# The sums of a graph layer's edge rows on TensorE: two places moved within a stage

## The chip, the cores and the metric

The kernel runs on one core of one Trainium2 chip. The metric is the time of one execution in device microseconds; the figure for the kernel before is the median of three runs. A core has five engines with a list of instructions each: PE (TensorE, matrix products, written to PSUM), DVE (VectorE), ACT (ScalarE), POOL (GpSimd) and SP (SyncE). SP issues most of the loads, POOL issues the indirect writes. The engines wait for each other through semaphores; each goes through its own list in order.

## The reference

A graph layer with 6250 nodes of 64 features and 206250 edges (100000 random ones in both directions, and a loop at each node), sorted by their target. Each edge has 64 features of its own. For each edge a two-layer network is applied to the features of one end and of the edge, the results are averaged over the edges of each source node (`row`), and a second network with a residual and a layer norm follows:

```python
msg = jnp.concatenate([src_node_features[col], edge_attr], axis=1)
h = jax.nn.relu(msg @ W1a.T + b1a)
h = h @ W1b.T + b1b
sums = jax.ops.segment_sum(h, row, num_segments=n_nodes)
...
agg = sums / jnp.maximum(counts, 1.0)[:, None]
z = jnp.concatenate([src_node_features, agg], axis=1)
z = jax.nn.relu(z @ W2a.T + b2a)
z = z @ W2b.T + b2b
out = jnp.concatenate([z, src_node_features], axis=1) @ Wr.T + br
...
x = _layernorm(x + out, axis=-1)
```

## The kernel before

The edges are padded to 1612 tiles of 128 and cut into 124 groups of 13 tiles. The source nodes fall into 49 bins of 128. The kernel sorts the hidden rows of the edges (128 values, a one for the count, and the node's place in its bin) by bin into a table in HBM, reads the table back bin by bin, and sums the rows of a bin with a one-hot matrix of the node numbers on PE. The second layer of the edge network is applied after the sum, since it is linear.

The main loop (`for k, ep_ in enumerate(epoch_of)`) has one **stage** for each group k. Several groups are in the making at once: in stage k the hidden rows of group k are computed, the places of group k+1 in the table are found, the one-hots of group k+2 are made, the inputs of group k+3 are loaded, and the rows of group k-2 are written.

In stages 8 to 103 a part of the group's tiles (6 of 13, or 9 in every other stage from 9 to 25) goes another way, the **joins**: three tiles at a time are first sorted within SBUF by a matmul with marks (one-hots of places), so that four rows of one bin lie side by side and can be written with one descriptor. Such a stage has two joins (or three). The names, with the lines of the profile:

- `counts_of(k+1)` on PE (L1092, L1093, L1096): how many edges of each bin stand ahead. It writes the PSUM tile `cnt_ps`.
- `hidden(k, ...)` on PE (L1353): first-layer rows of the tiles outside the joins, in two parts, `parts` and `last_part`. ACT takes them from PSUM (L1356) into `orow`.
- `join_bases(k+1)` on DVE (L1106 `of_quads`, L1110 `bases`): from the counts, the first place of each bin in the joins.
- `join_ranks(k+1)` on PE (L1119, L1121, L1122, L1127, L1131): the ranks of the next joins' edges. It needs `of_quads` and `bases`. The instructions `slots` (L1195, L1202), `join_at_slots` (L1143 `z_act`, L1144) and `join_places` (L1153, L1161, L1165) on DVE read what it left; in DVE's list they stand behind `marks`, `bins_of` and `side`, and L1195 is the first that waits for L1131.
- `marks(k, i)` on DVE (L1233) and ACT (L1238, L1239): the one-hots of join i. `side(k+1, ...)` on ACT (L1247) and DVE (L1250, L1254): the operands to be sorted.
- `join(k, i)` on PE (L1265), 6 matmuls of 512 columns: the sorting. ACT copies the result to SBUF (L1270 `rj`).
- `join_rows(k, i)` on PE (L1278): first-layer rows of the sorted edges; ACT takes them from PSUM (L1281). It needs `rj`. Between the copies and these evictions ACT's list has `columns(k+2, 1)` (L1318).
- `scatter(k-2)` on POOL (L1393 single rows, L1364 four rows at a time): the indirect writes. Some of them are made to wait for a matmul of the running stage (`pace`).
- `nodes_ahead`, `nodes_residual`, `nodes_load`, `nodes_store`: 17 small pieces of the node network, in stages 9 to 59, every third stage.

The **sums** of the table run while it is still being filled, on the part of each bin that is complete. Their work is cut into sum groups of up to three bins and twelve tiles, and `groups_at[k]` holds those of stage k: one, sometimes two, in a stage with joins. None is due before stage 29. A sum group goes through `issue` (the reads of the table, L1455 on SP, up to nine buffers ahead), `mark` (the one-hots, L1484 on DVE), and the matmuls of `summed` (L1503), into one PSUM tile (`h_ps`). `collect` adds the PSUM tile to `part` (L1563 on DVE, or for a bin's first sum a copy, L1561 on ACT), one sum group later. The first sum group of a stage is done in two pieces: `sum_first(k)` sums the first two of three bins, `sum_rest(k, g)` the other one, and then marks the next sum group and collects the last one. Further sum groups of the stage follow at its end with `sum_next(k)`. In the profile one f32 tile shows as two matmul records.

All tiles named `h_ps` share five PSUM buffers. The lists of PE, ACT, DVE and SP have the order in which the loop issues the instructions (`manual_schedule`); POOL's list is made by the compiler's scheduler. So on PE a stage with joins has the order: counts of k+1, first hidden rows of k, ranks of k+1, small node pieces, `sum_first`, last hidden rows, two joins, rows of the joins (with a third join between them where there is one), `sum_rest`, further sum groups.

Of the kernel before, what the change touches and what calls it, by code (L numbers as in the profile page):

```python
# [487 lines left out]
def fast_path(  # L488
# [64 lines left out]
    def joined(k):  # L553
        if not JOIN_FROM <= k < JOIN_TO:
            return 0
        return 3 if k in THRICE else 2
# [194 lines left out]
    with (  # L751
# [741 lines left out]
        def summed(st, reads, oh, of_bin, bins=None):  # L1493

            at_tile = 0
            for b0, nb, t0, n, rt in reads:
                for j in range(nb):
                    b = b0 + j
                    if bins and b not in bins:
                        at_tile += n  # L1500
                        continue
                    for t in range(n):
                        m = nc.tensor.matmul(  # L1503
                            of_bin(b), oh[:, at_tile, :], rt[:, j * n + t, : H + 1],
                            start=t0 + t == st.lo[b], stop=t0 + t == st.hi[b] - 1,
                        )
                        at_tile += 1
            return m.ins.name
# [36 lines left out]
        def mark():  # L1545

            if issued:
                g = issued.pop(0)
                g.oh = nodes_of(g.st, g.reads)
                marked.append(g)  # L1550
# [14 lines left out]
        def sum_first(k):  # L1565

            if not marked:
                mark()
            g = marked.pop(0)
            g.ps = hp.tile([P, SUMS, H + 1], F32, name="h_ps")  # L1570
            g.half = range(g.b0, g.b0 + -(-g.nb // 2))
            done[k, "first"] = summed(g.st, g.reads, g.oh, lambda b: g.ps[:, b - g.b0, :], g.half)
            return g

        def sum_rest(k, g):
            if g.nb > len(g.half):
                done[k, "rest"] = summed(
                    g.st, g.reads, g.oh, lambda b: g.ps[:, b - g.b0, :], range(g.half.stop, g.b0 + g.nb)
                )
            totals.append(g)  # L1580
            mark()
            collect(1)
            return g
# [27 lines left out]
        def issue(k):  # L1611

            while to_issue and sum(len(g.reads) for g in issued + marked) + len(to_issue[0][1]) <= READS:
                issued.append(Sums(k, *to_issue.pop(0)))
# [70 lines left out]
        for k, ep_ in enumerate(epoch_of):  # L1685
# [7 lines left out]
            due = len(issued) + len(marked) + len(to_issue)  # L1693
# [40 lines left out]
            if k + 2 < NGR:  # L1734
                columns(k + 2)
                ahead = bins_of(k + 2)
            if after:
                join_ranks(k + 1)
                side(k + 1, 1)
# [45 lines left out]
                nodes_load(nodes_at[k + 1])  # L1785
            if k in clears:
                clear(*clears[k])
            issue(k)

            g = sum_first(k) if due > 0 else None  # L1790
            if k + 1 < NGR:
                slots(k + 1, counts)
            if after:
# [6 lines left out]
                columns(k + 2, 1)  # L1800
            if after:
                join_places(k + 1)
            for i in range(joined(k)):
                join_rows(k, i)
                if i + 2 < joined(k):
                    join(k, i + 2)
            made.pop(k)
            if g:
                sum_rest(k, g)
                issue(k)  # L1810
            if k >= LEAD:
                scatter(k - LEAD)
            for i in range(1, due):
# [199 lines left out]
```

## Time and profile before

| | |
|---|---|
| median of 3 runs | 2145.13 us (2137.46 to 2148.65) |
| the profiled execution | 2149.18 us, of which the span of its instructions is 2147.2 us |
| mean granted clock of PE | 0.867 |
| PE, DVE, POOL, ACT busy | 76%, 63%, 54%, 51% of the span |
| stages 29 to 103 (joins and sums) | 448.2 to 1556.8 us of the span |

The page lists busy shares, the span in slices, the DMA queues, the chain of waits that ended last, and the groups of instructions of one line and shape. A group's row has the line and engine, the operation, the tile written and those read, the shape, the count, then busy time, the mean length in ns, and the idle time of that engine just before these instructions with what ended it. The timeline gives start, length, engine, line and, in brackets, the idle time before. The view of waits gives, for an engine and line, the instruction it waited for, the sum in us, how often and the longest. The windows give the same counts for a stretch of the span. "issue" and "remote" stand for waits whose end the profile does not show. Ends of matmuls are modelled, and a few records of matmuls are missing.

### The profile page before, as it was taken

What the parts mean: (1) busy time and instruction counts of PE and PEld (TensorE: products, weight loads), DVE (VectorE), ACT (ScalarE), POOL (GpSimd) and SP (SyncE); (2) the same over time, 40 slices, a digit from 0 to 9 for tenths busy, and PEclk for the clock granted to TensorE, in tenths of its full rate; (3) what the DMA queues carried; (4) which work ended last, traced back from release to release, by engine and by line L of the source; (5) the groups of instructions that cost most, each with busy time, mean ns of one, the idle gap of its engine ahead of it and who ended that gap; (6) DMA issues with size and microseconds to landing.
All of it is one profiled execution on the core that took longest, in us unless ns stands there. A gap on an engine that the chain in (4) does not pass through costs nothing.

```text
span 2147.2 us, 32795 instructions
## 1 busy us (share of the span) xinstructions
PE 1636.0 (76%) x10759; PEld 1443.4 (67%) x10759; DVE 1352.7 (63%) x3111; ACT 1087.4 (51%) x2203; POOL 1168.9 (54%) x1238
## 2 busy tenths in 40 slices
PE   4648776778888788888878878887767777777777
PEld 4536665667777677777767767776656666666666
DVE  7256666667766677767767767777645344454367
ACT  1237776766676566666666666666622222222015
POOL 5565565656665555556555565665654544545420
PEclk8568898999999999989998999999978777888889
DMA  7566666666765656555555555555677555565563
GB/s 183 151 204 201 214 226 209 232 210 208 226 206 182 199 174 199 171 150 183 176 157 157 170 159 175 180 172 162 196 224 219 165 173 165 171 187 162 159 180 104
DMA packets 227514, 394.09 MB, mean 184 GB/s; under 512 B 43228, under 2 KB 162527, under 8 KB 226951
## 3 DMA queue, kind: packets, MB, share of 16 engines
q1 hardware_dynamic: 152837, 224.58, 37.4%
q0 software_dynamic: 48368, 120.75, 16.2%
q10 hardware_dynamic: 26130, 46.58, 6.3%
q8 instruction: 88, 1.44, 0.3%
q14 instruction: 91, 0.75, 0.1%
HBM read 217.82 MB, written 173.91 MB: 182 GB/s over the span
## 4 chain that ended last, share of the span: by engine, by line
PE 59%; ACT 12%; issue 11%; another core or an unknown queue 9%; DVE 7%; DMA 2%; DVEq 0%; ACTq 0%; POOL 0%; SPq 0%; POOLq 0%
PE h_ps L1503 23%; PE h_ps L1353 10%; PE h_ps L1265 9%; PE h_ps L1278 8%; ACT orow L1356 2%; ACT rj L1270 2%; ACT rhs L1318 2%; ACT marks L1238 1%; ACT rhs L1316 1%; DVE marks L1233 1%; DMA rt<-rows 1%; PE cnt_ps L1092 1%; PE cnt_ps L1093 1%; ACT marks L1239 1%
## 5 line engine op out<-in xcount | busy, mean ns | idle before, releaser
L1393 POOL DMA_INDIRECT rows<-orow,rowidx x1009 | 973.1, 964 | 811.9 <-issue 211.3
L1503 PE MATMUL h_ps<-rt,oh 128*128 128x129 f32 x4014 | 601.9, 301 | 141.6 <-issue 135.7
L1503 PEld LDWEIGHTS h_ps<-rt,oh 128*128 128x128 f32 x4014 | 549.7, 214 | 170.9 <-issue 168.6
L1356 ACT ACTIVATE orow<-h_ps 128x384 f32<-128x384 f32 (+1 forms) x295 | 157.1, 536 | 727.1 <-PE h_ps L1353 501.1
L1278 PE MATMUL h_ps<-mv,rj 128*128 128x130 f32 x1608 | 260.9, 317 | 152.7 <-ACT rj L1270 98.3
L1278 PEld LDWEIGHTS h_ps<-mv,rj 128*128 128x128 f32 x1608 | 235.3, 220 | 191.8 <-ACT rj L1270 115.6
L1265 PE MATMUL h_ps<-marks,side 128*128 128x512 f32 x1206 | 322.5, 414 | 31.2 <-ACT orow L1356 10.3
L1353 PE MATMUL h_ps<-mv,rhs 124*128 124x128 f32 x2018 | 309.2, 301 | 33.5 <-issue 17.7
L1563 DVE TENSOR_TENSOR part<-part,h_ps 128x387 f32<-128x387 f32 (+2 forms) x219 | 111.6, 510 | 352.1 <-remote 172.4
L1484 DVE TENSOR_TENSOR oh<-ramp,rt 128x768 f32<-128x768 bf16 (+3 forms) x428 | 315.0, 775 | 4.6 <-DMA rt<-rows 4.6
L1353 PEld LDWEIGHTS h_ps<-mv,rhs 124*128 124x128 f32 x2018 | 280.0, 213 | 41.0 <-issue 21.6
L1265 PEld LDWEIGHTS h_ps<-marks,side 128*128 128x128 f32 x1206 | 227.8, 197 | 84.9 <-ACT orow L1356 12.3
L1233 DVE TENSOR_TENSOR marks<-quad_ramp,ramp 128x1024 fp32r<-128x1024 f32 x201 | 241.2, 1204 | 0.0
L1364 POOL DMA_INDIRECT quads<-orow,qidx x201 | 192.8, 959 | 78.5 <-issue 36.9
L1281 ACT ACTIVATE orow<-h_ps 128x260 f32<-128x260 f32 x402 | 138.5, 388 | 69.5 <-PE h_ps L1278 32.6
L1270 ACT COPY rj<-h_ps 128x512 f32<-128x512 f32 x201 | 113.8, 588 | 111.1 <-PE h_ps L1265 67.9
L1106 DVE TENSOR_SCALAR of_quads<-cnt_ps 128x98 bf16<-128x98 f32 x96 | 25.5, 266 | 229.1 <-PE cnt_ps L1096 84.5
L1239 ACT ACTIVATE marks<-marks,ones 128x512 fp32r<-128x512 f32 x201 | 145.2, 722 | 6.6
L1050 DVE TENSOR_TENSOR_SCAN had<-ramp,bins 128x400 bf16<-128x400 bf16 (+1 forms) x124 | 137.5, 1109 | 12.4 <-issue 0.3
L1238 ACT ACTIVATE marks<-quad_ramp,z_act 128x512 fp32r<-128x512 f32 x201 | 143.7, 715 | 0.0
L1316 ACT ACTIVATE rhs<-rhs,from_win 60x896 f32<-60x896 bf16 (+1 forms) x116 | 130.4, 1124 | 2.9
L1318 ACT ACTIVATE rhs<-rhs,ones 60x896 f32<-60x896 f32 (+1 forms) x116 | 130.2, 1123 | 2.9
(188 smaller groups left out, 1505.0 us busy)
## 6 DMA issues: line engine op xcount, KB each, us to landing
rt<-quads SPq DMA_DIRECT2D x113, 390.0 KB
rt<-rows SPq DMA_DIRECT2D x100, 390.0 KB
rt<-rows SPq DMA_DIRECT2D x115, 195.0 KB
rhs<-in_edgeT SPq DMA_DIRECT2D x87, 224.0 KB
enat<-in_edgeJ SPq DMA_DIRECT2D x87, 192.0 KB
rows<-orow,rowidx POOLq DMA_INDIRECT x1009
quads<-padrow ACTq DMA_DIRECT2D x12, 1300.0 KB
rt<-rows SPq DMA_DIRECT2D x45, 325.0 KB
```

Of the source, the lines that this page charges most:

```text
L1233: nc.vector.tensor_tensor(m[:, :n, :], all_q[:, None, :].to_broadcast([P, n, QUAD * P]), z[:, :n, None].to_broadcast([P, n, QUAD * P]), op ...
L1238: nc.scalar.activation(m[:, t, :], all_q, AF.Square, bias=z_acts[k][:, i * JOIN + t : i * JOIN + t + 1], scale=-1.0)
L1239: nc.scalar.activation(m[:, t, :], m[:, t, :], AF.Relu, bias=ones[:, :1], scale=-1.0)
L1265: nc.tensor.matmul(ps, s[:, p, i * JOIN + t, :], m[:, t, :], start=t + p == 0, stop=t == JOIN - 1 and p == 1,)
L1278: done[k, f"join{i}"] = nc.tensor.matmul(ps[:, j, :], rj[:, (g0 + j) * P : (g0 + j + 1) * P], m, start=True, stop=True).ins.name
L1318: nc.scalar.activation(rhs[D:WIDE, :], rhs[D:WIDE, :], AF.Relu, bias=ones[D:WIDE, :1], scale=-1.0)
L1353: done[k, c] = nc.tensor.matmul(ps[:, j, :], rhs[:WIDE, of * P : (of + 1) * P], m[:WIDE, :H], start=True, stop=True).ins.name
L1356: nc.scalar.activation(orow_of(k, k0, n)[:, :, :H], ps[:, :n, :], AF.Relu)
L1364: s = nc.gpsimd.indirect_dma_start(out=qep.rows.rearrange("(q r) f -> q (r f)", r=QUAD), out_offset=bass.IndirectOffsetOnAxis(ap=qidx[:, q ...
L1393: s = nc.gpsimd.indirect_dma_start(out=ep_.rows, out_offset=bass.IndirectOffsetOnAxis(ap=rowidx[:, k % RING * BLK + j : k % RING * BLK + j ...
L1484: nc.vector.tensor_tensor(res[:, at_tile : at_tile + nb * n, :], ramp[:, None, :].to_broadcast([P, nb * n, P]), node[:, :, None].to_broadc ...
L1503: m = nc.tensor.matmul(of_bin(b), oh[:, at_tile, :], rt[:, j * n + t, : H + 1], start=t0 + t == st.lo[b], stop=t0 + t == st.hi[b] - 1,)
```

## The change

Three calls move within a stage; no other line changes. The first reads of the sums (`issue(k)`) and `sum_first(k)` go from behind the node pieces to ahead of the next joins' ranks. `sum_rest(k, g)`, with the marking and collecting in it, and the second `issue(k)` go from behind the joins' rows to between the first two joins and their rows.

```diff
                 columns(k + 2)
                 ahead = bins_of(k + 2)
+            issue(k)
+            g = sum_first(k) if due > 0 else None
             if after:
                 join_ranks(k + 1)
                 side(k + 1, 1)
...
             if k in clears:
                 clear(*clears[k])
-            issue(k)
-
-            g = sum_first(k) if due > 0 else None
             if k + 1 < NGR:
                 slots(k + 1, counts)
...
             if after:
                 join_places(k + 1)
+            if g:
+                sum_rest(k, g)
+                issue(k)
             for i in range(joined(k)):
                 join_rows(k, i)
                 if i + 2 < joined(k):
                     join(k, i + 2)
             made.pop(k)
-            if g:
-                sum_rest(k, g)
-                issue(k)
             if k >= LEAD:
                 scatter(k - LEAD)
```

On PE the order of a stage with joins becomes: counts of k+1, first hidden rows of k, `sum_first`, ranks of k+1, node pieces, last hidden rows, two joins, `sum_rest`, rows of the joins, further sum groups. In stages without joins PE's order is the same as before. On DVE the order stays but for the first stage with a sum, where the one-hots come ahead of L1250 and L1254. On ACT the copies L1561 come ahead of that stage's evictions L1281. On SP the reads L1455 come ahead of the node pieces' loads and stores. On POOL four pairs of neighbouring writes change places.

## The prediction

> **What bounds the kernel now.** I read the page first: busy shares, then the chain of waits.
>
> ```profile
> span 2147.2 us, 32795 instructions
> ...
> PE 1636.0 (76%) x10759; PEld 1443.4 (67%) x10759; DVE 1352.7 (63%) x3111; ACT 1087.4 (51%) x2203; POOL 1168.9 (54%) x1238
> ...
> PE 59%; ACT 12%; issue 11%; another core or an unknown queue 9%; DVE 7%; DMA 2%; DVEq 0%; ACTq 0%; POOL 0%; SPq 0%; POOLq 0%
> ```
>
> PE carries 59% of the chain and is busy 76% of the span. An average says nothing about where a moved matmul matters, so next I asked in which stretch the moved instructions (L1503) and the joins' ranks (L1119) run together. Columns: window, length, PE busy (count), PEld busy, granted clock, DMA share, GB/s. The first three rows hold L1503 alone, the fourth all engines.
>
> ```profile
> 0.00:448.20 448.20, 0.00 (x0) 0.00 (x0) 0.81 0.66 206
> 448.20:1556.80 1108.60, 272.78 (x1924) 255.14 (x1924) 0.93 0.59 180
> 1556.80:2147.20 590.40, 329.15 (x2092) 294.54 (x2091) 0.80 0.59 173
> ```
>
> ```profile
> 448.20:1556.80 1108.60, 904.95 (x6204) 800.55 (x6202) 790.17 (x1882) 702.28 (x1384) 659.09 (x686) 0.93 0.59 180
> ```
>
> No sums run before 448.2 (stage 29), and after 1556.8 (stage 104 on) there are no joins, so nothing stands between the two new places and the old ones: hidden rows follow the first bins and other bins follow the hidden rows in both orders. Only 1108.6 us, 75 stages of 14.8 us, can change. PE is idle there for 1108.6 - 904.95 = 203.7 us. The groups of instructions name what it waited in front of (last part of a row: idle time before it, and its causes):
>
> ```profile
> L1278 PE MATMUL h_ps<-mv,rj 128*128 128x130 f32 x1202 | 195.4, 314 | 111.7 <-ACT rj L1270 58.4 <-issue 24.1 <-ACT orow L1281 20.2
> L1119 PE MATMUL cnt_ps<-joh,before_w 128*128 128x300 bf16 x74 | 22.6, 305 | 48.0 <-DVE of_quads L1106 45.0 <-issue 2.6
> L1503 PE MATMUL h_ps<-rt,oh 128*128 128x129 f32 x1924 | 273.0, 297 | 6.9 <-issue 6.6 <-ACT orow L1281 0.3
> ```
>
> So 111.7 + 48.0 = 159.7 of the 203.7 us stand exactly at the two places to which sums are moved, and the sums themselves almost never wait for their data (6.9 us). One stage on PE's timeline (start, length, then the idle time before):
>
> ```profile
> 1022.71 1.12 PE L1353 MATMUL h_ps<-mv,rhs 124*128 124x128 f32 x8
> 1025.37 0.29 PE L1119 MATMUL cnt_ps<-joh,before_w 128*128 128x300 bf16 x1 [1.53 <-DVE of_quads L1106]
> ...
> 1026.19 1.59 PE L1503 MATMUL h_ps<-rt,oh 128*128 128x129 f32 x12
> 1027.61 0.83 PE L1353 MATMUL h_ps<-mv,rhs 124*128 124x128 f32 x6
> 1028.20 2.99 PE L1265 MATMUL h_ps<-marks,side 128*128 128x512 f32 x12
> 1031.03 1.55 PE L1278 MATMUL h_ps<-mv,rj 128*128 128x130 f32 x12
> 1033.34 0.71 PE L1278 MATMUL h_ps<-mv,rj 128*128 128x130 f32 x4 [0.76 <-ACT rhs L1318]
> 1033.89 0.83 PE L1503 MATMUL h_ps<-rt,oh 128*128 128x129 f32 x6
> 1034.56 0.33 PE L1092 MATMUL cnt_ps<-had,one_w 128*128 128x400 bf16 x1
> ```
>
> PE goes through its list in order: it stands for DVE's `of_quads` with 12 sum matmuls ready behind the ranks, and for ACT with 6 ready behind the rows.
>
> **The change part by part.** No instruction is added or removed.
>
> *First bins in front of the ranks.* They occupy PE from 1026.19 to the next start, 1027.61: 1.42 us. In front of L1119 that covers each wait up to 1.42 us. The waits, by releaser (sum, times, longest):
>
> ```profile
> PE cnt_ps L1119 <- DVE of_quads L1106: 45.0, 31, 3.9
> PE h_ps L1278 <- ACT rj L1270: 58.4, 29, 3.9
> PE h_ps L1278 <- ACT orow L1281: 20.2, 29, 0.8
> ```
>
> With the 2.6 us put to "issue" there are 48.0 us in some 33 waits. Upper bound: 33 x 1.42 = 47. Lower bound, if all were 3.9 or nothing: 48.0 / 3.9 = 12 waits x 1.42 = 17. The mean wait (1.45) is about the cover; I take 34.
>
> *Other bins between joins and rows.* From 1033.89 to 1034.56: 0.67 us. The rows' end is set by ACT (the copy L1270, then L1318, then the evictions L1281), counted from the joins' end, so it stays where it is and the next stage starts 0.67 us sooner wherever ACT makes PE wait at least that long. The 29 waits for L1270 (mean 2.0) and the 29 for L1281 (mean 0.70) give 58 x 0.67 = 39; every one of 75 stages would give 50. I take 45.
>
> *Sum and what is left of it.* 34 + 45 = 79 us (56 to 97 by the bounds). Not all of it arrives, for a stage cannot get shorter than what the other engines need. In the window DVE has 790.17 / 75 = 10.5 us a stage, ACT 9.4, and POOL:
>
> ```profile
> 1031.28 0.96 POOL L1393 DMA_INDIRECT rows<-orow,rowidx  x1 [0.31 <-issue]
> ```
>
> 0.96 + 0.31 = 1.27 us an instruction, 686 of them: 871 us, 11.6 a stage. The mean stage (14.8) has room for 1.05 us; the short one above (12.3) has not, and where a late `rj` also holds back the evictions the next wait grows. I take 0.6 of 79: 47 us; the ends for the range are 0 and 1.
>
> *Clock.* PE's rows show a second price of standing still:
>
> ```profile
> 1098.20 0.41 PE L1119 MATMUL cnt_ps<-joh,before_w 128*128 128x300 bf16 x1 [2.36 <-DVE of_quads L1106]
> ...
> 1099.27 2.93 PE L1503 MATMUL h_ps<-rt,oh 128*128 128x129 f32 x12
> 1101.99 1.49 PE L1353 MATMUL h_ps<-mv,rhs 124*128 124x128 f32 x6
> ```
>
> Behind that stop the same 12 matmuls take 2.72 us, not 1.42. Over the window the grant is 0.93, so (1 - 0.93) x 1108.6 = 78 us are lost. The stops become shorter, but a stop of 3.9 us only by 1.42 or 0.67; I take 10 of the 78 (0 to 60). The Trainium skill ("TensorE: Matmul & The Clock Gate", "What's actually happening") gives the rule: one idle window of about 3.4 us halves the clock, and it is binary. The factor of 1.9 in these rows agrees; that a shorter stop of 2.36 us was enough differs from a plain threshold, since the window may lie anywhere.
>
> *What is pushed back.* (a) In the 74 - 33 = 41 stages without a wait at L1119 the ranks now start 1.42 us later. DVE's L1195 waits for the last rank matmul (L1131), and behind it in DVE's list stand `z_act`, `join_places`, the one-hots and the next marks.
>
> ```profile
> 1009.53 0.18 PE L1131 MATMUL cnt_ps<-of_quads,more_w 128*128 128x50 bf16 x1
> 1013.30 0.52 DVE L1195 TENSOR_REDUCE row<-cnt_ps 128x7 f32<-128x350 f32 x1
> L1195 DVE TENSOR_REDUCE row<-cnt_ps 128x7 f32<-128x350 f32 (+1 forms) x76 | 39.8, 524 | 16.2 <-PE h_ps L1265 9.1 <-remote 4.7 <-issue 2.4
> ```
>
> DVE comes 3.6 us after the ranks; 2.2 would remain: nothing lost, though if that cover were gone it would cost 41 x 1.42 = 58 us. (b) The first ACT copies of 17 sum groups (L1561) come in front of the row evictions:
>
> ```profile
> L1561 ACT COPY part<-h_ps 128x387 f32<-128x387 f32 (+1 forms) x17 | 7.7, 469 | 4.9 <-PE h_ps L1353 3.5 <-PE h_ps L1503 1.4
> ```
>
> at most 7.7 us; the 0.67 us of sums cover most, I take 2. (c) On SP the reads for the sums come in front of the node groups' loads and stores (17 each); nobody waits for the stores, the reads come sooner: 0, within 3 us either way. (d) POOL's list keeps its order but for four neighbouring pairs: 0. (e) In stages with two sum groups DVE's addition L1563 waits for the other bins, which now end before the rows:
>
> ```profile
> 1023.45 0.56 DVE L1563 TENSOR_TENSOR part<-part,h_ps 128x387 f32<-128x387 f32 x1 [4.62 <-PE cnt_ps L1096]
> ```
>
> That wait was what made the marks and `of_quads` late for 1025.37. It helps where the cover is too short, at most the 48 - 34 = 14 us left there; I take 0.
>
> Total 47 + 10 - 2 = 55. The profiled execution took 2149.18 us (span 2147.2 and 2.0 around it): 2094. The median of the runs is 4 us lower than it, 2145.13, so I forecast **2090 us**.
>
> **The rivals.** *Nothing arrives:* the waits turn up again further on (at L1353 for PSUM, at L1265 for marks), because ACT and POOL, not PE, pace the stages. For it: POOL's 11.6 us, the chain's 12% ACT and 9% unknown. Against: those engines are idle for a fifth or more of each stage. With a tenth of the 55 us left: 2140. Chance 0.13.
>
> *The clock stays up:* with the stops cut, most of the 78 us come back: 60 in place of 10, 2040. For it: the two rows of L1503, a factor of 1.9. Against: the stops of 2 to 4 us lose only 0.67 or 1.42. By the rule of the Trainium skill just named a longest stop of 3.9 - 0.67 = 3.2 us falls short of a window. Chance 0.12.
>
> *Slower:* the ranks in the 41 stages come too late for DVE. PE's signals sometimes arrive long after the matmul: L1356 wants the hidden rows of 1010.98 and starts at 1016.02.
>
> ```profile
> 1010.98 0.83 PE L1353 MATMUL h_ps<-mv,rhs 124*128 124x128 f32 x6
> 1016.02 0.49 ACT L1356 ACTIVATE orow<-h_ps 128x384 f32<-128x384 f32 x1 [2.06 <-PE h_ps L1265]
> ```
>
> From the point where the ranks' signal is over 2.2 us late the delay goes through DVE's list into the next joins. Price up to 58, less 0.6 x 45 = 27 still gained at the rows: 2145 + 31 = 2176. Against: only 16.2 us of waiting at L1195 today. Chance 0.18.
>
> That the change does not do what it says is excluded: the changed program has the moved matmuls in the new places in all 75 stages.
>
> **How the numbers follow.** Forecast 0.57 (its own range 2065 to 2120), nothing 0.13, clock 0.12, slower 0.18. Range 2038 to 2160: it holds the forecast, the second case and parts of the two outer ones, with under 0.2 outside. About 0.5%, 11 us, is what this kernel's runs can tell from no change: below 2134 lie the forecast and the clock, less a tail, 0.68; 2134 to 2156 holds "nothing" and a little of its neighbours, 0.14; above, 0.18.
>
> **What would show it.** Right: idle before L1119 falls from 48.0 to under 20, before L1278 from 111.7 to about 70, the window to stage 104 is some 55 us shorter and the time after it is still 590 us. Clock: a grant over 0.93 in the window. Wrong: idle before L1195 well over 16.2 us (the slower rival), or new idle time before L1353, L1265 or L1503 that adds up to what L1119 and L1278 lost.

## The result and the profile after

The changed kernel is slower by 1%: its median is 2162.27 us against 2141.3 us for the kernel before, run beside it, ratio 1.0104 with a 95% interval of 1.0067 to 1.0140. One of its six runs, at 2867.64 us, lies far above the others and is left out of the ratio. The profiled execution of the changed kernel (2154.23 us) is its fastest run, while that of the kernel before (2149.18 us) is above all its timed runs, so the two traces differ by 5 us only, and their parts say more than their sums.

The windows of the changed kernel, cut where the sums begin and at the same place behind stage 104 as before (window, length, busy time of PE, PEld, DVE, ACT, POOL with counts, granted clock, DMA share, GB/s):

```profile
0.00:449.00 449.00, 302.30 (x1718) 254.86 (x1719) 268.76 (x679) 242.57 (x492) 260.49 (x292) 0.79 0.65 205
449.00:1565.70 1116.70, 917.36 (x6214) 809.38 (x6212) 790.90 (x1882) 697.38 (x1383) 659.89 (x686) 0.91 0.58 178
1565.70:2152.40 586.70, 435.05 (x2832) 393.24 (x2830) 293.21 (x552) 145.31 (x330) 249.94 (x261) 0.79 0.59 175
...
449.00:1554.30 1105.30, 908.69 (x6150) 802.08 (x6148) 784.78 (x1872) 693.25 (x1374) 653.19 (x679) 0.91 0.58 178
```

The middle window was to get 55 us shorter and got 8 us longer (1108.6 before). It holds stage 104 too; from here on "the stages" are exactly 29 to 103 (fourth row), which took 1097.2 us before and 1105.3 us after. The outer windows moved by less than 4 us. The groups of these stages in the changed kernel (busy, mean ns, then idle time before them and its causes):

```profile
L1278 PE MATMUL h_ps<-mv,rj 128*128 128x130 f32 x1202 | 196.3, 313 | 125.7 <-ACT rj L1270 80.4 <-issue 25.9 <-ACT orow L1281 15.2
L1265 PE MATMUL h_ps<-marks,side 128*128 128x512 f32 x900 | 247.2, 424 | 45.0 <-DVE xr_now L1660 14.6 <-DVE nz L1652 9.1 <-ACT xr_now L1653 7.9
L1119 PE MATMUL cnt_ps<-joh,before_w 128*128 128x300 bf16 x74 | 22.1, 299 | 11.1 <-DVE of_quads L1106 8.2 <-issue 2.8
L1270 ACT COPY rj<-h_ps 128x512 f32<-128x512 f32 x150 | 83.9, 588 | 129.5 <-PE h_ps L1265 51.3 <-remote 40.3 <-PE h_ps L1278 31.3
L1195 DVE TENSOR_REDUCE row<-cnt_ps 128x7 f32<-128x350 f32 x74 | 38.2, 516 | 74.7 <-PE h_ps L1265 30.6 <-remote 26.4 <-PE h_ps L1503 15.5
```

Two of these rows and the window of just these stages were not shown for the kernel before; there they read:

```profile
448.20:1545.40 1097.20, 896.79 (x6150) 793.01 (x6148) 783.66 (x1870) 697.61 (x1378) 653.02 (x679) 0.93 0.58 179
...
L1265 PE MATMUL h_ps<-marks,side 128*128 128x512 f32 x900 | 236.7, 411 | 28.4 <-ACT orow L1356 10.3 <-ACT xr_now L1653 9.0 <-DVE xr_now L1660 3.4
L1270 ACT COPY rj<-h_ps 128x512 f32<-128x512 f32 x150 | 85.7, 587 | 95.0 <-PE h_ps L1265 55.3 <-remote 19.2 <-issue 11.2
```

The wait in front of the ranks is covered as forecast: 48.0 to 11.1 us at L1119. It came back at the joins: L1278 rose from 111.7 to 125.7 instead of falling to 70, because ACT's copy L1270, which it waits for, itself waits 129.5 us in place of 95.0, and L1265 rose from 28.4 to 45.0. And PE's own instructions got longer: the grant fell from 0.93 to 0.91, and with the same 6150 records of matmuls PE is busy 908.7 us in these stages, before 896.8. These 12 us, less the 4 us by which PE's idle time fell, are the 8 us that the stages got longer.

**What L1270 waits for.** The trace also has the times of PE's semaphore increments, called signals here. I matched them in order to the matmuls that carry one. Most arrive 0.01 to 0.04 us after the recorded end, but many arrive microseconds later. A stage of the first experiment below (only the first bins moved) shows it on the timeline:

```profile
589.02 1.50 PE L1503 MATMUL h_ps<-rt,oh 128*128 128x129 f32 x12
...
591.60 2.99 PE L1265 MATMUL h_ps<-marks,side 128*128 128x512 f32 x12
591.61 0.96 POOL L1393 DMA_INDIRECT rows<-orow,rowidx  x1 [1.25 <-PE cnt_ps L1131]
...
592.87 0.96 POOL L1393 DMA_INDIRECT rows<-orow,rowidx  x1 [0.30 <-issue]
...
594.13 1.17 POOL L1393 DMA_INDIRECT rows<-orow,rowidx  x1 [0.30 <-issue]
...
595.61 0.96 POOL L1393 DMA_INDIRECT rows<-orow,rowidx  x1 [0.30 <-PE h_ps L1265]
...
595.95 1.16 PE L1278 MATMUL h_ps<-mv,rj 128*128 128x130 f32 x8 [1.35 <-issue]
...
596.88 0.96 POOL L1393 DMA_INDIRECT rows<-orow,rowidx  x1 [0.30 <-issue]
...
598.91 0.59 ACT L1270 COPY rj<-h_ps 128x512 f32<-128x512 f32 x1 [3.02 <-remote]
...
599.55 1.06 PE L1278 MATMUL h_ps<-mv,rj 128*128 128x130 f32 x4 [2.45 <-ACT rj L1270]
```

The second join ends at 594.60; its signal comes at 598.89, ACT starts at 598.91 after 3.02 us of standing, and PE stands 2.45 us. The signals of the first eight matmuls of the rows, done at 596.66 and 597.11, come 0.06 and 0.12 us behind it, at 598.95 and 599.01: the signals had queued up and are let go together. Meanwhile POOL issued one indirect write after the other, 1.26 to 1.48 us apart; the release follows 1.05 us after the last of them ended at 597.84.

In every profile I then counted, over the stages, a signal as late if it came over 0.6 us after its matmul and no earlier one was still pending, against the number of POOL's indirect writes begun in the 3.6 us ahead of that matmul's end. Four of the profiles:

| kernel | stages, us | joins' signals late | late after at most 1 write | after 2 | after 3 or more |
|---|---|---|---|---|---|
| before | 1097.2 | 14 of 82 | 0 of 80 | 40 of 320 | 93 of 139 |
| changed | 1105.3 | 35 of 72 | 0 of 132 | 71 of 245 | 91 of 120 |
| e1_first | 1130.2 | 39 of 80 | 0 of 147 | 31 of 250 | 108 of 142 |
| e2_rest | 1095.9 | 20 of 76 | 0 of 110 | 39 of 258 | 94 of 128 |

In these four no signal is late after at most one write, and after three or more at least two in three are; in the other profiles a few are late after at most one, the most (4 of 104) in `e11_after_pace2`. Not every signal is in the trace (669 for the 810 matmuls that carry one, in these stages of the kernel before), so the counts depend on how the gaps are bridged. Bridged another way, the first row reads 0 of 79, 44 of 319 and 83 of 138, and the joins' signals are late in 32 of 101 cases before and 41 of 88 after the change: the step from one write to three stands, the shares of the joins are rough.

The Trainium skill ("Perfetto Trace Analysis", "Per-instruction lifecycle: what the profiler-reported window actually captures") says that a matmul's reported end is an estimate, and that its semaphore update is pushed only when PSUM has acknowledged the bytes. The order of the two in the trace agrees: an ordinary signal here follows the reported end by 0.01 to 0.04 us. The 4.29 us above are over a hundred times that.

### The profile page after: what moved, and what is told of

Read it like the earlier page. It is cut to its first block, busy times and chain, and to the rows that moved or that the text cites. A ratio compares the mean times of both kernels' runs of the same rounds, so it can differ in the third digit from the quotient of the medians.

```text
span 2152.4 us, 32807 instructions
## 1 busy us (share of the span) xinstructions
PE 1654.7 (77%) x10759; PEld 1457.5 (68%) x10759; DVE 1352.9 (63%) x3111; ACT 1085.3 (50%) x2203; POOL 1170.3 (54%) x1238
## 4 chain that ended last, share of the span: by engine, by line
PE 58%; ACT 13%; issue 13%; another core or an unknown queue 8%; DVE 5%; DMA 2%; SPq 1%; ACTq 0%; DVEq 0%; POOL 0%; POOLq 0%
PE h_ps L1503 22%; PE h_ps L1353 9%; PE h_ps L1265 9%; PE h_ps L1278 9%; ACT rj L1270 2%; ACT orow L1356 2%; ACT rhs L1318 2%; ACT rhs L1316 2%; ACT marks L1238 2%; PE cnt_ps L1092 1%; PE cnt_ps L1093 1%; ACT orow L1281 1%; PE h_ps L879 1%; ACT marks L1239 1%
## 5 line engine op out<-in xcount | busy, mean ns | idle before, releaser
L1503 PE MATMUL h_ps<-rt,oh 128*128 128x129 f32 x4014 | 603.3, 299 | 140.5 <-issue 132.7
L1503 PEld LDWEIGHTS h_ps<-rt,oh 128*128 128x128 f32 x4014 | 557.8, 213 | 179.6 <-issue 164.4
L1278 PE MATMUL h_ps<-mv,rj 128*128 128x130 f32 x1608 | 262.4, 316 | 160.0 <-ACT rj L1270 110.5
L1265 PE MATMUL h_ps<-marks,side 128*128 128x512 f32 x1206 | 334.8, 426 | 51.1 <-DVE xr_now L1660 14.6
L1278 PEld LDWEIGHTS h_ps<-mv,rj 128*128 128x128 f32 x1608 | 229.3, 219 | 194.5 <-ACT rj L1270 126.2
L1353 PE MATMUL h_ps<-mv,rhs 124*128 124x128 f32 x2018 | 321.4, 310 | 26.0 <-issue 19.7
L1353 PEld LDWEIGHTS h_ps<-mv,rhs 124*128 124x128 f32 x2018 | 287.1, 219 | 33.3 <-issue 23.3
L1265 PEld LDWEIGHTS h_ps<-marks,side 128*128 128x128 f32 x1206 | 234.9, 204 | 108.2 <-DVE xr_now L1660 17.1
L1281 ACT ACTIVATE orow<-h_ps 128x260 f32<-128x260 f32 x402 | 139.9, 388 | 99.3 <-PE h_ps L1278 32.2
L1270 ACT COPY rj<-h_ps 128x512 f32<-128x512 f32 x201 | 112.3, 589 | 146.0 <-PE h_ps L1265 64.4
```

The lines of the kernel that those rows point to most:

```text
L1265: nc.tensor.matmul(ps, s[:, p, i * JOIN + t, :], m[:, t, :], start=t + p == 0, stop=t == JOIN - 1 and p == 1,)
L1278: done[k, f"join{i}"] = nc.tensor.matmul(ps[:, j, :], rj[:, (g0 + j) * P : (g0 + j + 1) * P], m, start=True, stop=True).ins.name
L1353: done[k, c] = nc.tensor.matmul(ps[:, j, :], rhs[:WIDE, of * P : (of + 1) * P], m[:WIDE, :H], start=True, stop=True).ins.name
L1503: m = nc.tensor.matmul(of_bin(b), oh[:, at_tile, :], rt[:, j * n + t, : H + 1], start=t0 + t == st.lo[b], stop=t0 + t == st.hi[b] - 1,)
```

## The experiments

The kernels ran in sets on several chips, and each ratio is against the kernel before on the same chip. Theory S is the slower rival of the prediction; B, M, P and Q are told where they come up. A diff below shows the lines that matter, with `...` for lines left out.

**1. The halves of the change.** The first bins alone, `e1_first`:

```diff
+            issue(k)
+            g = sum_first(k) if due > 0 else None
             if after:
                 join_ranks(k + 1)
...
-            issue(k)
-
-            g = sum_first(k) if due > 0 else None
             if k + 1 < NGR:
                 slots(k + 1, counts)
```

> Only the first half of the change: the first reads and sum_first stand ahead of the next joins' ranks, the other bins stay behind the joins' rows. Theory S (the slower rival of the prediction: the ranks come too late for DVE, and the delay goes on through z_act, the one-hots and the marks): this half carries the loss, ratio 1.01 to 1.02 against before (2160 to 2180 us), idle before L1195 about 70 us as in the changed kernel. Theory B (the other bins behind the joins hold back the copies of the joins, L1270): this half alone gains what L1119 lost, ratio 0.98 to 0.99 (2100 to 2125 us), although L1195 waits.

The other bins alone, `e2_rest`:

```diff
+            if g:
+                sum_rest(k, g)
+                issue(k)
             for i in range(joined(k)):
                 join_rows(k, i)
...
-            if g:
-                sum_rest(k, g)
-                issue(k)
             if k >= LEAD:
                 scatter(k - LEAD)
```

> Only the second half of the change: sum_rest, with its marks and collection, and the second issue stand between the joins and their rows, sum_first stays behind the ranks. Theory S: this half gains, ratio 0.985 to 0.995 (2110 to 2130 us), idle before L1278 falls to about 70 to 90 us, L1195 stays near 16. Theory B: ratio 1.005 to 1.02 (2150 to 2180 us), ACT starts L1270 later after the joins' last matmul, and the idle time before L1278 does not fall.

`e3_first_pe` is the first of these with `issue(k)` left at its old place:

```diff
+            g = sum_first(k) if due > 0 else None
             if after:
                 join_ranks(k + 1)
...
-            issue(k)
-
-            g = sum_first(k) if due > 0 else None
+            issue(k, [g] if g else [])
```

> As the first run, but the first reads on SP (L1455) stay at their old place and only the matmuls of sum_first stand ahead of the ranks. If the reads' earlier place costs nothing, as the prediction had it (0, within 3 us), this run and the first agree within 0.4%. If the earlier reads hold up the node pieces' loads, this one is faster than the first by 0.5% or more, and the idle time before L1265 for L1652, L1653 and L1660 is smaller.

and `e4_rest_pe` the second with its marks, collection and reads left behind the rows:

```diff
+            if g:
+                sum_other(k, g)
             for i in range(joined(k)):
                 join_rows(k, i)
...
             if g:
-                sum_rest(k, g)
+                sum_rest(k, g, False)
                 issue(k)
```

> As the second run, but only the matmuls of the other bins stand between the joins and their rows; the marking, the collection and the second issue stay behind the rows, in the order of the kernel before on DVE, ACT and SP. Theory B blames the matmuls alone: same ratio as the second run within 0.4%. If the earlier one-hots, copies and reads are what matters, this run differs from the second one by 0.5% or more and L1563 waits 80 us again instead of under 10.

Measured: e1 1.0142 (1.0093 to 1.0190), e3 1.0161 (1.0115 to 1.0207), e2 0.9994 (0.9959 to 1.0030), e4 1.0011 (0.9970 to 1.0051). The first half carries the loss, its matmuls alone; the reads on SP and the order on DVE cost nothing that can be told; the second half gains nothing. The ratio of e1 is the one that S forecast, but the place of the loss is not, and the ratio of e2 lies in the band of neither theory. The groups of e1 in the stages:

```profile
L1278 PE MATMUL h_ps<-mv,rj 128*128 128x130 f32 x1202 | 213.7, 332 | 153.2 <-ACT rj L1270 96.6 <-issue 34.0 <-ACT orow L1281 20.9
L1270 ACT COPY rj<-h_ps 128x512 f32<-128x512 f32 x150 | 84.6, 587 | 161.3 <-remote 78.6 <-PE h_ps L1265 49.6 <-PE h_ps L1278 27.2
L1195 DVE TENSOR_REDUCE row<-cnt_ps 128x7 f32<-128x350 f32 x74 | 38.0, 513 | 34.5 <-PE h_ps L1265 26.4 <-remote 5.7 <-PE cnt_ps L1131 2.5
L1119 PE MATMUL cnt_ps<-joh,before_w 128*128 128x300 bf16 x74 | 21.8, 295 | 12.7 <-DVE of_quads L1106 10.3 <-issue 2.1
```

L1119 gives 35 us, L1278 takes 42 back and the copies L1270 wait 66 us more, while L1195, where S saw the loss, waits 18 us more and not 54. Theory B is refuted too: the copies are late without any other bins behind the joins. What is late are the joins' signals, 39 of 80 in place of 14 of 82. In e1 35 of the 75 stages have three or more writes begun in the 3.6 us before the last join's end, in the kernel before 17, in the changed kernel 40. In e2 there are 30 such stages, and 20 of 76 joins' signals are late: this half brings joins among the writes too. Rows of e2:

```profile
L1503 PE MATMUL h_ps<-rt,oh 128*128 128x129 f32 x1900 | 272.3, 292 | 18.9 <-issue 18.6 <-DMA rt<-rows 0.3
L1265 PE MATMUL h_ps<-marks,side 128*128 128x512 f32 x900 | 243.9, 415 | 43.5 <-issue 21.1 <-DVE xr_now L1660 8.6 <-ACT xr_now L1653 7.9
L1278 PE MATMUL h_ps<-mv,rj 128*128 128x130 f32 x1202 | 186.9, 305 | 79.8 <-ACT rj L1270 49.1 <-ACT orow L1281 12.2 <-issue 11.9
L1119 PE MATMUL cnt_ps<-joh,before_w 128*128 128x300 bf16 x74 | 22.4, 303 | 54.6 <-DVE of_quads L1106 49.8 <-issue 4.8
```

L1278 fell by 32 us as hoped, and L1265, L1503 and L1119 rose by 15, 12 and 7.

**2. Without POOL's indirect writes.** Theory P: POOL's indirect writes, issued back to back, hold up PE's signals, and the change puts the joins' signals among them. In `e5_before_direct` and `e6_after_direct` the single rows of the stages are written by SP, to a place of their own. A part that is not shown here lets the sums read the first table's rows from another array:

```diff
             for j in range(j0, BLK):
                 t = k * BLK + j
+                if 29 <= k + LEAD <= 103:
+                    nc.sync.dma_start(aside[state["spare"] * P : (state["spare"] + 1) * P, :], orow_of(k, j)[:, 0, :])
+                    state["spare"] += 1
+                    continue
```

> The kernel before, with POOL's single-row indirect writes (L1393) of the stages with sums taken away: each is replaced by a plain write of the same 128 rows to a place of its own, issued by SP, so the bytes and the rows written stay, and the first table's reads take rows of the same shape from another array (the sums are left meaningless). Theory P: PE's signals arrive late when POOL issues indirect writes back to back (in the kernel before, of the signals with at most one such write begun in the 3.6 us ahead 0 of 81 were over 0.6 us late, with three or more 66% were). Then here the late signals all but vanish (under 5% of the joins' signals over 0.6 us late, before 18%), and idle before L1278 and L1119 changes with them. Theory M (the writes' traffic, or PE's own density, makes them late): the share stays within a third of before.

> The changed kernel with the same replacement of POOL's single-row writes. Theory P, which puts the loss of the change down to late signals of the joins: without them the gain that was forecast appears, this one is 25 to 60 us (1.2 to 3%) faster than the kernel before with the same replacement. If the order itself is at fault (the ranks pushed back delay z_act and the marks), this one is as slow as or slower than the other, as with the indirect writes.

With the sums meaningless the kernel's general path ran behind the fast one, so the whole times (7731.45 and 7694.67 us) cannot be set beside the others, and the stages are compared, in one profile of each. The window of the stages and two groups, first for e5, then for e6 (L1279 and L1120 are L1278 and L1119, one line further down):

```profile
448.80:1326.40 877.60, 812.35 (x6150) 733.26 (x6149) 777.51 (x1872) 697.96 (x1380) 155.16 (x162) 0.99 0.81 225
...
L1279 PE MATMUL h_ps<-mv,rj 128*128 128x130 f32 x1201 | 170.1, 285 | 57.1 <-ACT orow L1282 47.2 <-ACT rj L1271 7.0 <-DVE part L1574 2.6
L1120 PE MATMUL cnt_ps<-joh,before_w 128*128 128x300 bf16 x74 | 21.9, 296 | 0.2
```

```profile
445.30:1286.50 841.20, 807.55 (x6151) 730.76 (x6149) 773.94 (x1872) 693.82 (x1380) 155.28 (x162) 0.99 0.82 234
...
L1279 PE MATMUL h_ps<-mv,rj 128*128 128x130 f32 x1202 | 167.6, 284 | 24.2 <-ACT rj L1271 9.7 <-ACT orow L1282 3.6 <-ACT part L1572 3.3
```

No signal of a join is late (0 of 150 and 0 of 149), the stages take 877.6 us in place of 1097.2, and now the order of the change is the faster one by 36.4 us; the whole times differ by as much, 36.8. M is refuted: the DMA engines move 225 GB/s in place of 179, PE is denser, and the signals are punctual. But POOL was also idle, so a theory Q, by which POOL's mere time and waits pace the stages, was open. To tell it apart small memsets keep POOL busy for each write, with the write's waits; twelve in `e9_before_busy` and `e10_after_busy`, seven in `e13_before_busy7` and `e14_after_busy7`:

```diff
+                    s = nc.gpsimd.memset(busy, 0.0)
+                    for _ in range(6):
+                        nc.gpsimd.memset(busy, 0.0)
```

> The kernel before with POOL's single-row writes of the stages with sums issued by SP to a place of their own, as in the run e5_before_direct, and POOL kept busy in their place: twelve small memsets for each write (about 1.2 to 1.4 us), with the same waits for PE (the first table's reads take rows of another array, so the sums are left meaningless). Theory P (indirect writes hold up PE's signals): the signals stay punctual, under 5% of the joins' signals late, and stages 29 to 103 take 850 to 950 us, far under the 1097 of the kernel before. Theory Q (POOL is simply the engine that paces the stages, by its time and its waits): with POOL as busy as before they take 1050 us or more.

> The changed kernel with the same replacement and the same busy POOL. Theory P: 20 to 50 us shorter over stages 29 to 103 than e9_before_busy, as the prediction wanted and as with the plain writes alone (841 against 878 us). Theory Q: within 10 us of it or longer.

> As e9_before_busy, whose twelve memsets took 2.1 us for each write in place of 1.27 us, so that POOL became the bound: now seven memsets, about 1.2 us, so POOL is as busy as with the writes (single-row writes by SP, reads from another array, sums meaningless). Theory P (the indirect writes hold up PE's signals): joins' signals punctual, stages 29 to 103 in 860 to 950 us, idle before L1278 under 100 us. Theory Q (POOL's time paces the stages): 1050 us or more.

> The changed kernel in the same form. Theory P: 20 to 50 us shorter over stages 29 to 103 than e13_before_busy7. Theory Q: within 10 us of it or longer.

Twelve were too many: 2.1 us for each write made POOL the bound, and the stages took 1182.9 and 1166.2 us. That is the time that Q expected, yet no join's signal is late (0 of 145 in e9); e10's 16.7 us less lie between the two expectations. What the bound looks like in the view of waits of e9 (of PE, then of ACT; L1280, L1283 for L1278, L1281; sum in us, times, longest):

```profile
PE h_ps L1280 <- ACT orow L1283: 224.2, 64, 8.5
...
ACT orow L1283 <- DMA quads<-orow,qidx: 249.8, 103, 10.8
```

PE waits for the evictions, and these for buffers that POOL has not written out. In the kernel before PE's wait is 20.2 us and in the changed one 15.2, and none of ACT's waits there is put down to a DMA, so POOL's rate was not what stopped them. With seven, POOL's timeline in e13 shows 1.23 us for each write, near its 1.27:

```profile
700.64 0.12 POOL L1398 MEMSET busy<- 128x24 f32 x1
700.82 1.00 POOL L1400 MEMSET busy<- 128x24 f32 x6
701.87 0.12 POOL L1398 MEMSET busy<- 128x24 f32 x1
```

The window of the stages and the rows of L1280, for e13 and then for e14:

```profile
449.30:1329.60 880.30, 811.21 (x6150) 732.79 (x6149) 776.95 (x1871) 697.39 (x1378) 580.39 (x3768) 0.99 0.83 223
...
L1280 PE MATMUL h_ps<-mv,rj 128*128 128x130 f32 x1201 | 171.2, 287 | 60.8 <-ACT orow L1283 46.7 <-ACT rj L1272 10.5 <-DVE part L1585 2.3
```

```profile
443.00:1299.00 856.00, 812.12 (x6151) 734.75 (x6149) 775.93 (x1874) 694.32 (x1381) 566.67 (x3700) 0.99 0.84 230
...
L1280 PE MATMUL h_ps<-mv,rj 128*128 128x130 f32 x1202 | 169.6, 286 | 31.0 <-ACT rj L1272 15.2 <-ACT part L1583 3.3 <-ACT orow L1283 3.2
```

880.3 and 856.0 us, no join's signal late (0 of 138, 0 of 142): Q is refuted. It is the indirect writes, not POOL's time, that made the signals late, and with punctual signals the change gains 24 to 36 us.

The reads from another array are not what makes the signals punctual. In stages 8 to 27 no sum reads the table yet, and POOL issues all its indirect writes in these kernels too. There, after three or more writes, 22 of 46 signals are late in the kernel before, 18 of 40 in e5 and 18 of 47 in e13: the same executions, on the same chips, have late signals first and none at the joins of stages 29 to 103. The four-row writes stay in those stages too, and of the signals with two of them ahead some are late (9 of 144 in e5, 21 of 118 in e13).

**3. Other places for the writes.** These keep all writes and move what they wait for. `e7_after_pace` and `e8_before_pace` change the line of `pace` for stages with two joins (`"join0"` and `"join1"` are the rows L1278 of the two joins) and let the first four-row write wait for the counts:

```diff
-                else {6: 9, 8: BLK - 1, 10: "join0", 12: "join1"} if j0 == 2 * JOIN
+                else {6: 9, 7: "ranks", 8: BLK - 1, 9: "join0", 10: "join1", 12: "rows"} if j0 == 2 * JOIN
```

> The changed kernel with another pacing of POOL's writes in stages with two joins: the first write of four rows waits for the counts, single rows 6 to 12 wait as 6: first hidden rows, 7: ranks, 8: last hidden rows, 9: rows of join 0, 10 on: rows of join 1 (was 6: first hidden rows, 8: last hidden rows, 10 and 12: rows of joins 0 and 1). One write instead of two falls between the last hidden rows and the joins' end. Theory P: the joins' signals are late less often (under 25% over 0.6 us against 49% in the changed kernel), idle before L1278 falls from 125.7 to under 100, and the time falls by 10 to 40 us against the changed kernel, unless the five writes then bunched behind the rows make the counts' and hidden rows' signals late instead (idle before L1119 or ACT's wait at L1356 rises by as much). Theory S (late ranks): no change within 0.5%.

> The kernel before with the same new pacing. Theory P: here the joins' signals were late in 18% only, so less is to be won there, and the bunched writes make the signals of counts and first hidden rows late, in front of which PE stands uncovered: 0 to 1.5% slower than before. Theory S: no change within 0.5%.

e7 0.9949 (0.9914 to 0.9984), e8 0.9951 (0.9915 to 0.9987) of the kernel before: the change that cost 1% costs nothing with this pacing. The time fell as P expected, but by another road: 16 of 57 joins' signals are late, just over the expected share, yet the idle time before the rows is still 122.9 us, where under 100 was expected. e8, for which P saw a loss, gained as much, so with this pacing the order makes no difference (2101.54 and 2102.38 us). `e11_after_pace2` only moves the release of rows 8 and 9:

```diff
-                else {6: 9, 8: BLK - 1, 10: "join0", 12: "join1"} if j0 == 2 * JOIN
+                else {6: 9, 8: "join0", 12: "join1"} if j0 == 2 * JOIN
```

> The changed kernel, with one wait of POOL's writes moved: in stages with two joins rows 8 and 9 wait for the rows of join 0 in place of the last hidden rows, so no write is released between the last hidden rows and the end of the joins. Theory P: under 15% of the joins' signals over 0.6 us late, idle before L1278 below 100 us; the writes then run seven in a row from the rows on, so signals of counts and first hidden rows are late and part of it is lost there: 0 to 1.5% faster than the changed kernel. Theory Q: later writes make POOL later, 0.5% or more slower than the changed kernel.

1.0112 (1.0070 to 1.0155), 45 of 83 joins' signals late: a miss. In 45 of its 75 stages three or more writes still begin in the 3.6 us before the last join's end. Rows 8 and 9 of the stage now wait for rows behind that join and cannot be among them, so earlier ones had moved in. One place cannot be emptied by one wait when nine writes of 1.27 us take 11.4 us of a stage of 14.6. `e12_after_pace3` spreads the waits over more writes (the four-row writes wait too), and `e15_after_pace3_late` and `e16_after_pace_late` have the pacing of e12 and of e7 in the stages with sums alone; the line of e15:

```diff
-                {9: BLK - 1, 10: "join0", 11: "join1", 12: "join2"} if j0 == 3 * JOIN
+                {6: "ranks", 7: BLK - 1, 8: "rest", 9: "join0", 10: "join1"} if 29 <= k + LEAD < JOIN_TO
+                else {9: BLK - 1, 10: "join0", 11: "join1", 12: "join2"} if j0 == 3 * JOIN
```

> The changed kernel with POOL's writes spread further: the two writes of four rows wait for counts and first hidden rows, single row 6 for the ranks, 7 for the last hidden rows, 8 for the other bins, 9 and 10 for the rows of joins 0 and 1. Theory P: fewer runs of three or more writes, so fewer late signals than in e7_after_pace and 0 to 1% faster than that one, or, where a wait on a late signal holds POOL back, the same within 0.5%. Theory Q: more waits make POOL later, slower than e7_after_pace by 0.5% or more.

> The changed kernel with the spread pacing of e12_after_pace3 in stages 29 to 103 alone: in e12 these stages took 1080 us against 1105 in the changed kernel, but stages 8 to 28, which have no sums to cover anything, took 322 us against 293. Theory P: joins' signals late in about 30% again and the time 0.97 to 0.995 of the kernel before. If the spacing of the writes was not what shortened these stages, 1.00 to 1.012 as in the changed kernel and in e12.

> The changed kernel with the pacing of e7_after_pace in stages 29 to 103 alone. If e7's gain of 1.5% over the changed kernel comes from the stages to which the change applies, the ratio against before is 0.99 to 1.00 again; if it came from stages 8 to 28, it is 1.005 to 1.012, as in the changed kernel.

e12 1.0022 (0.9991 to 1.0054), e15 0.9921 (0.9879 to 0.9964), e16 0.9980 (0.9931 to 1.0030). e12 is a miss as well: P had it as fast as e7 or faster, and it is 0.7% slower, as Q had it. Its stages with sums took 1079.6 us, but stages 8 to 28 took 322 us against 293 in the changed kernel. e15, without that loss, beats both kernels; 15 of 80 of its joins' signals are late. Its window of the stages and the rows' group:

```profile
444.10:1523.40 1079.30, 897.12 (x6150) 793.68 (x6148) 784.63 (x1877) 698.18 (x1376) 656.81 (x684) 0.92 0.59 184
...
L1280 PE MATMUL h_ps<-mv,rj 128*128 128x130 f32 x1202 | 179.8, 294 | 102.0 <-issue 69.6 <-ACT orow L1283 19.4 <-ACT rj L1272 9.4
```

The wait for `rj` has gone from 80.4 to 9.4 us. 1079.3 is far from 856, though, and the idle time before the rows is still 102.0 us: of the rows' signals 172 of 271 now come over 0.6 us late, queued ones counted, against 71 of 270 in the changed kernel. That this is cheaper because only evictions wait for them is argued, not shown. The ratio of e16 lies in the band set for a gain from the stages with sums, but the median of all its twelve runs, 2149.16 us against 2146.7, lies just above that band, so the time decides little. Its profile says more: these stages take 1088.8 us, near the 1086.2 of e7 and not the 1105.3 of the changed kernel.

**4. The order with spread writes.** `e17_before_pace3_late` has the order before and the pacing of e15 as far as it fits, `e18_rest_pace3_late` the second half of the change with exactly that pacing.

> The order of the kernel before with POOL's writes spread out in stages 29 to 103 as in e15_after_pace3_late, as far as that order allows: four-row writes at counts and first hidden rows, row 6 at the ranks, 7 at the first bins, 8 at the last hidden rows, 9 and 10 at the rows of joins 0 and 1. If the spread writes alone made e15's gain (0.992), this one has 0.99 to 0.995 too. If the change's order gains once the writes are spread, this one is at 0.995 to 1.005.

> Only the second half of the change (other bins between the joins and their rows, first bins behind the ranks), with exactly the pacing of e15_after_pace3_late in stages 29 to 103. Against e15 (0.992) it differs by the first half alone. If that half, which cost 1.4% with the old pacing, costs nothing or gains with this one, this run is at 0.992 to 1.005; if it still costs, this one is faster, 0.98 to 0.987.

This pair ran on another chip, and there the kernel before itself took 1657.46 us (2115.68 to 2148.49 on the chips of the other experiments). The changed kernel itself was not run there. e17 is at 1.0023 (1.0014 to 1.0032), e18 at 0.9948 (0.9932 to 0.9963). The chain's shares by engine in e17, then the window of its stages and three groups (L1403 is the indirect write, L1280 and L1120 are L1278 and L1119):

```profile
PE 53%; DMA 16%; ACT 12%; issue 7%; DVE 7%; POOL 4%; ACTq 0%; DVEq 0%; SPq 0%; POOLq 0%
```

```profile
349.10:1222.00 872.90, 809.56 (x6150) 732.82 (x6149) 779.64 (x1878) 699.58 (x1380) 648.88 (x674) 1.00 0.74 226
...
L1403 POOL DMA_INDIRECT rows<-orow,rowidx x524 | 506.2, 966 | 164.6 <-issue 89.0 <-PE h_ps L1280 12.7 <-PE h_ps L1513 11.3
L1280 PE MATMUL h_ps<-mv,rj 128*128 128x130 f32 x1202 | 171.4, 286 | 55.5 <-ACT orow L1283 48.6 <-DVE part L1573 4.0 <-ACT rj L1272 2.6
L1120 PE MATMUL cnt_ps<-joh,before_w 128*128 128x300 bf16 x74 | 21.9, 296 | 0.3 <-DVE of_quads L1107 0.2
```

The indirect writes are as many and as long as ever (966 ns), 702 signals have three or more of them ahead, and none of 878 is late. The stages take 872.9 us with the order before, as in e5 and e13. So the question that the pair was made for (the first half's price with spread but late signals) is not answered. But it repeats the other finding with all writes in place: against e17, e18 has 26.5 us of idle time before the rows in place of 55.5, its stages take 859.0 us, and it is 0.8% faster (1647.76 / 1661.23 = 0.992):

```profile
348.60:1207.60 859.00, 814.85 (x6150) 732.46 (x6148) 777.90 (x1879) 694.03 (x1380) 645.88 (x672) 0.99 0.76 230
...
L1280 PE MATMUL h_ps<-mv,rj 128*128 128x130 f32 x1202 | 168.6, 285 | 26.5 <-ACT rj L1272 10.3 <-ACT orow L1283 7.8 <-ACT part L1571 3.1
```

It also differs from e17 in the waits of rows 7 and 8, so this is not the order alone. POOL has little room left there: 671 indirect writes at 1.27 us each would be 852 of the 859 us, an estimate from the spacing in the kernel before.

## Why the prediction was wrong, point by point

*First bins in front of the ranks* (34 us, 17 to 47): the cover itself worked, 37 us here and 35 in e1. What was wrong is that the wait was treated as PE's own loss. With punctual signals it does not exist (0.2 us in e5, 0.8 in e13, 0.3 in e17): `of_quads` was late because the counts' signals were. Covered there, PE runs up to 1.4 us ahead, and more of its joins end within a run of POOL's writes (three or more of them ahead of the last join's end in 40 of 75 stages, before in 17). The wait moves to L1270 and L1278, where nothing covers it.

*Other bins between joins and rows* (45 us): 32 us at L1278 in e2, given back at L1265, L1503 and L1119. With punctual signals about the same saving, 30 to 33 us at that line, stays (60.8 to 31.0 between e13 and e14, 57.1 to 24.2 between e5 and e6).

*Sum and what is left of it* (0.6 of 79 = 47 us): this is the step that failed. It let a share of the waits vanish because other engines pace the stages, but had no term for signals that come late because POOL writes, which turned the covered waits into new ones. Measured: nothing arrives, the stages get 8 us longer and 1% is lost. Without late signals 24 to 36 us arrive, about the 0.6 x 45 = 27 us that the step left to the second half.

*Clock* (10 us gained): the grant fell from 0.93 to 0.91 and the same matmuls took 12 us more. PE still stands 196.6 us in the stages (1105.3 less 908.7) against 200.4. With punctual signals the grant is 0.99. So the rival in which the clock stays up did not come either: the wait it needs to lose was still there.

*What is pushed back.* (a) The ranks: 0 was wrong for the row (L1195 16.2 to 74.7) but not for the time, since e1 has the whole loss with 34.5. (c) The reads: right, e1 and e3 agree. (d) POOL: its list hardly changed, and that was read as nothing to pay; what changed is where its writes fall against PE's signals. (e) The collection's wait fell from 83.0 to 6.4 us in the middle window, as said, and brought nothing. (b) was too small to be seen.

*The rivals.* The slower one came true in sign and size (2176 forecast, 2162 measured) and in its means, late signals of PE, but not in its place: the joins, not the ranks. That its size fits is luck, since it was worked out from a delay at the ranks (58 us) that e1 does not have. Its "against", only 16.2 us at L1195, looked at the wrong consumer. The view that spoke for it was already quoted: 9% of the chain released by "another core or an unknown queue", which on the chip of e17 is not there.

Still open: why the same writes make signals late on the other chips and not on that of e17 and e18, what the change itself would do on that chip, and what holds the signals (whether the release waits for POOL to pause or only happens then).

## What to carry to other kernels

Before filling a wait, look at why the thing waited for is late: compare the recorded end of the producer with the start of the consumer, and where they differ by microseconds ask what else runs then, on engines that neither of them uses. The gap in front of the ranks, which late signals had caused, did not go away when work was put into it; it moved behind that work. Where POOL issues indirect writes, their pacing against the signals on the path is a knob of its own: the changed kernel stood at 1.010 of the kernel before, and with e15's pacing, on another chip, at 0.992.

## What the runs showed of the hardware

PE's semaphore updates came microseconds late, 4.29 us in the stage shown, when POOL issued indirect writes every 1.3 us, and queued updates then arrived 0.06 us apart; with at most one such write in the 3.6 us before, 0 of 80 were late in the kernel before. Memsets of the same length on POOL together with plain writes of the same rows issued by SP do not do this (0 of 138 joins' signals late in e13). On the chip of e17 the indirect writes do not either: 702 signals have three or more ahead, and none is late. There the stages of e17 take 224 us less than in the profile of the kernel before (872.9 against 1097.2), about what the plain writes won on another chip (1097.2 - 877.6 = 220): in these stages the difference between the chips has the size of what the late signals cost.
